# A four-layer image network: convolution copies, convolution taps, scan states and an elementwise sum change engines in its last layer

## The chip, the cores and the metric

The kernel runs on one core of a Trainium2 chip. The metric is the device time of one execution in microseconds (us), lower is better, given as the median of several runs. A core has five engines that run their own instruction streams side by side and wait for each other on semaphores: PE (TensorE, matrix products), DVE (VectorE), ACT (ScalarE), POOL (GpSimd) and SP (SyncE, which here issues DMAs). Data sits in SBUF (128 partitions), products land in PSUM, and DMA moves data between SBUF and device memory.

## The reference

The input is x of shape (2, 128, 128, 128), as batch, height, width and channels, in fp32. Four residual layers follow one another, each of the form x = x + layer(norm(x)). The first is windowed attention, the second a Fourier layer with a feed-forward part, the third a recurrent spectral layer of 16 steps. The change lies in the fourth, a selective-scan layer. Cut down, it computes:

```python
def layer3(x):                                  # x is already normalised
    xc, z = split(x @ W_in.T)                   # 256 channels each
    xc = silu(depthwise_conv3x3(xc, conv_w) + conv_b)
    # four sequences of 16384 pixels: 16 windows of 32 x 32, walked by
    # rows, by columns, and both of these backwards
    xs = stack([rows(xc), cols(xc), rows(xc)[::-1], cols(xc)[::-1]])
    dt, B, C = split(x_proj_w @ xs)             # 8, 16 and 16 rows
    delta = softplus(dt_proj_w @ dt + dt_proj_b)
    h = 0                                       # 256 channels x 16 states per sequence
    for t in range(16384):                      # for each of 2 batches x 4 directions
        h = exp(delta[t] * A) * h + delta[t] * xs[t] * B[t]
        y[t] = (h * C[t]).sum(over states) + xs[t] * Ds
    y = y_rows + y_rows_back + y_cols + y_cols_back    # each put back in pixel order
    y = layernorm(y) * ln_w + ln_b
    return (y * silu(z)) @ W_out.T
```

## The kernel before

Everything is fp32. The fourth layer has three stages, one after another, each with its own pools of tiles; a pool's number is how many buffers a tile name has, and a tile that needs a buffer waits until its last user is done.

**Convolution, `layer3_conv`.** It loops over 2 batches x 4 blocks of 32 image rows (`hg`), eight blocks in all. The order of instructions on each engine in this stage is chosen by the framework's scheduler. For a block, SP loads rows of the layer's input (`x3l`, L1141), and ACT normalises them into `xpad`, a padded tile of 34 rows by 130 columns. Then for each half of the 256 channels (`e` = 0, 1): PE multiplies by the input projection `win` (`zps`) and ACT copies the result into `xz`, again padded. The nine offsets ("taps") of the 3x3 convolution are split. Taps 0 to 2 are done by PE: their weights are folded into the projection, `cw` = conv_w x win, so a product of `cw` with the shifted `xpad` gives the projected tap (`cps`, L1172, two matmuls of 512 columns a tap). Taps 3 to 8 are done by DVE, each with one `scalar_tensor_tensor` over 128x1024 (L1181), the first of them adding to `cps` and the others to `acc`. There are four such groups (`g`, 8 rows each) for a block and half. ACT applies bias and silu into `xw` (L1185), which is stored by windows (`wg`, four for a block). Last, for each window, three things leave for device memory: `xw` in row order (`xs[0]`), a copy in column order `xv` (`xs[1]`), and a transposed copy `xt` (`xst`) that PE makes with transposes (`xtps`, L1207) and ACT copies out of PSUM (L1212). The column-order copy is L1194, on POOL, 128x1024, two for a window, 64 in all; it reads with a stride of 32 elements. `cps`, `xv`, `xt` and `xtps` have two buffers each, `acc`, `xz` and `xw` three.

**Scan, `layer3_scan`.** The sequences are cut into 256 parts, eight chains of 32 parts (2 batches x 4 directions), and a part into 8 slots, so 2048 slots (`g`), each with four scans of 512 steps. The order of instructions is written out by hand (`with in_order(tc)`): on turn `g` the loop calls `exponentials(g + 1)` (ACT, `da`, L1531), `kept(g - 1)` (ACT copies the last states, L1610), `products(g + 2)` (`but`, on ACT and POOL), `weighted(g - 1)` (POOL multiplies by C, L1616), `tiles(g)` (PE transposes into `ups`, DVE scans, L1598) and `sums(g - 2)` (PE, L1569). `tiles` starts each chain by making a state tile and clearing it:

```python
            if (b, k) not in states:
                states[(b, k)] = two.tile([P, 32], F32, name=f"state_{b}_{k}", tag="state")
                nc.gpsimd.memset(states[(b, k)], 0.0)
```

The call of `weighted(g - 1)` comes ahead of `tiles(g)`, so the clearing (L1582) stands behind that multiplication in POOL's order.

**Output, `layer3_out`.** 64 tiles of four image rows (512 pixels), order again written by hand. On turn `m` it calls, in this order: `load(m + 4)`, `join(m + 2)`, `project(m - 1)`, `weigh(m)`, `gate(m + 1)`, `norm(m + 1)`, `normal(m + 2)`. `load` fetches the tile's input and two scan sums `y` and `y2`, six buffers each. `join` adds the two in place (L1681, POOL, 128x1024). `norm` is the layer norm: statistics on DVE (L1708, L1710), the reciprocal root on POOL (`rsqrt_of`, L51 and L52), and then subtracting and scaling on DVE in four instructions of 128x256 (L1714). `weigh` transposes on PE (`yTp`, L1725), scales on ACT (L1728) and multiplies by the gate on DVE (L1732). `gate` computes silu(z) (L1697 on PE, L1700 on ACT), `project` multiplies by W_out and adds the residual (L1741, L1743), and ACT copies the result out (L1747) and issues its store.

Of the kernel before, what the change touches and what calls it, by code (L numbers as in the profile page):

```python
# [9 lines left out]
F32 = mybir.dt.float32  # L10
AF = mybir.ActivationFunctionType
ALU = mybir.AluOpType
# [3 lines left out]
P = 128  # L16
NB = 2
# [10 lines left out]
def rows_of(handle, n, offset=0):  # L28

    return bass.AP(handle.tensor, handle.offset + offset, [[0, P], [1, n]])  # L30
# [1063 lines left out]
def layer3_conv(tc, cs, ins, x3, xs, xst, sc, sh):  # L1094

    nc = tc.nc
    MAT = (0, 1, 2)
    VEC = (3, 4, 5, 6, 7, 8)
    with ExitStack() as ctx:
        pool = lambda name, bufs, **kw: ctx.enter_context(tc.tile_pool(name=name, bufs=bufs, **kw))
        w = pool("l3a_w", 1)
        two = pool("l3a_two", 2)
        three = pool("l3a_three", 3)
        ps_t = pool("l3a_ps_t", 2, space=PSUM)  # L1110
        ps_z = pool("l3a_ps_z", 2, space=PSUM)
        ps_c = pool("l3a_ps_c", 2, space=PSUM)
        win = w.tile([P, 256], F32, name="win")
        nc.sync.dma_start(win, ins["winT"][:, 0:256])

        cw = w.tile([P, len(MAT), 256], F32, name="cw")
        nc.sync.dma_start(cw.rearrange("p t e -> p (t e)"), rows_of(ins["conv_w_t"], len(MAT) * 256))

        cv = w.tile([P, 9, 2], F32, name="cv")
        nc.sync.dma_start(cv.rearrange("p t e -> p (t e)"), cols_of(ins["conv_w_t"], 9 * 256))  # L1120
        cb = w.tile([P, 2], F32, name="cb")
        nc.sync.dma_start(cb, cols_of(ins["L3_conv_conv_b"], 256))
        nc.vector.tensor_tensor(
            cw, cw, win.unsqueeze(1).to_broadcast([P, len(MAT), 256]), ALU.mult
        )
        for b in range(NB):
            for hg in range(4):
                xpad = two.tile([P, 34, 130], F32, name=f"xpad_{b}_{hg}", tag="xpad")
                nc.gpsimd.memset(xpad[:, :, 0:1], 0.0)  # L1129
                nc.gpsimd.memset(xpad[:, :, 129:130], 0.0)  # L1130
                if hg == 0:
                    nc.gpsimd.memset(xpad[:, 0:1, 1:129], 0.0)
                if hg == 3:
                    nc.gpsimd.memset(xpad[:, 33:34, 1:129], 0.0)
                r = max(32 * hg - 1, 0)
                end = min(32 * hg + 33, HW)
                while r < end:
                    n = min(8, end - r)
                    xl = two.tile([P, 8, HW], F32, name=f"x3l_{b}_{hg}_{r}", tag="x3l")
                    nc.sync.dma_start(  # L1140
                        xl[:, 0:n, :].rearrange("c r w -> c (r w)"), x3[b, :, r * HW : (r + n) * HW]  # L1141
                    )
                    p0 = r - 32 * hg + 1
                    nc.scalar.activation(
                        xpad[:, p0 : p0 + n, 1:129], xl[:, 0:n, :], AF.Identity,
                        bias=sh[:, b : b + 1], scale=sc[:, b : b + 1],
                    )
                    r += n
                xw = []
                for e in range(2):  # L1150
                    t = f"{b}_{hg}_{e}"
                    ep = slice(e * P, (e + 1) * P)
                    xz = three.tile([P, 34, 130], F32, name=f"xz_{t}", tag="xz")
                    nc.gpsimd.memset(xz[:, :, 0:1], 0.0)
                    nc.gpsimd.memset(xz[:, :, 129:130], 0.0)
                    for r in range(0, 34, 4):
                        n = min(4, 34 - r)
                        zps = ps_z.tile([P, 4, HW], F32, name=f"zps_{t}_{r}", tag="zps")
                        nc.tensor.matmul(
                            zps[:, 0:n, :], win[:, ep], xpad[:, r : r + n, 1:129],  # L1160
                            start=True, stop=True,
                        )
                        nc.scalar.copy(xz[:, r : r + n, 1:129], zps[:, 0:n, :])
                    xwe = three.tile([P, 4, 32, 32], F32, name=f"xw_{t}", tag="xw")
                    xw.append(xwe)
                    for g in range(4):
                        cps = ps_c.tile([P, 8, HW], F32, name=f"cps_{t}_{g}", tag="cps")
                        for i, tap in enumerate(MAT):
                            dy, dx = tap // 3, tap % 3
                            for h in range(2):  # L1170
                                r = 8 * g + 4 * h + dy
                                nc.tensor.matmul(  # L1172
                                    cps[:, 4 * h : 4 * h + 4, :], cw[:, i, ep],
                                    xpad[:, r : r + 4, dx : dx + HW],
                                    start=(i == 0), stop=(i == len(MAT) - 1),
                                )
                        acc = three.tile([P, 8, HW], F32, name=f"acc_{t}_{g}", tag="acc")
                        for i, tap in enumerate(VEC):
                            dy, dx = tap // 3, tap % 3
                            r = 8 * g + dy  # L1180
                            nc.vector.scalar_tensor_tensor(  # L1181
                                acc, xz[:, r : r + 8, dx : dx + HW], cv[:, tap, e : e + 1],
                                cps if i == 0 else acc, ALU.mult, ALU.add,
                            )
                        nc.scalar.activation(  # L1185
                            xwe[:, :, 8 * g : 8 * g + 8, :].rearrange("p g r w -> p r g w"),
                            acc.rearrange("p r (g w) -> p r g w", w=32),
                            AF.Silu, bias=cb[:, e : e + 1],
                        )
                for wg in range(4):  # L1190
                    t = f"{b}_{hg}_{wg}"
                    xv = two.tile([P, 2, 32, 32], F32, name=f"xv_{t}", tag="xv")
                    for e in range(2):
                        nc.gpsimd.tensor_copy(xv[:, e], xw[e][:, wg].rearrange("p h w -> p w h"))  # L1194
                        nc.sync.dma_start(
                            xs[0, b, hg, wg, :, e, :], xw[e][:, wg].rearrange("p h w -> p (h w)")
                        )
                        nc.sync.dma_start(
                            xs[1, b, hg, wg, :, e, :], xv[:, e].rearrange("p w h -> p (w h)")
                        )  # L1200
                    xt = two.tile([P, 8, 256], F32, name=f"xt_{t}", tag="xt")
                    for g in range(4):
                        tps = ps_t.tile([P, 2, 2, P], F32, name=f"xtps_{t}_{g}", tag="x3t")
                        for j in range(2):
                            for e in range(2):
                                h0 = 4 * (2 * g + j)
                                nc.tensor.transpose(  # L1207
                                    tps[:, j, e, :],
                                    xw[e][:, wg, h0 : h0 + 4, :].rearrange("p h w -> p (h w)"),
                                    cs.ident,  # L1210
                                )
                        nc.scalar.copy(  # L1212
                            xt[:, 2 * g : 2 * g + 2, :], tps.rearrange("p j e d -> p j (e d)")
                        )
                    nc.sync.dma_start(xst[b, hg, wg].rearrange("(t p) d -> p t d", p=P), xt)


def layer3_scan(tc, cs, ins, xs, xst, yc, ys):
# [11 lines left out]
    nc = tc.nc  # L1230
    NS, DR, NX, T = 16, 8, 40, 512
    with ExitStack() as ctx:
        pool = lambda name, bufs, **kw: ctx.enter_context(tc.tile_pool(name=name, bufs=bufs, **kw))
        w = pool("l3b_w", 1)
        one = pool("l3b_one", 1)
        two = pool("l3b_two", 2)
# [19 lines left out]
        for i in range(2):  # L1256
            t = w.tile([65, T], F32, name=f"xd{i}")
# [18 lines left out]
            for s in (range(15, -1, -1) if back else range(16))  # L1276
            for sub in ((1, 0) if back else (0, 1))
        ]
        states = {}
        held = {}  # L1280

        def tag_of(i):
# [291 lines left out]
        def tiles(g):  # L1574
            i, s = divmod(g, 8)
            q, e = divmod(s, 2)
            b, k, _, _ = parts[i]
            rev = k >= 2
            v = held[i]
            if (b, k) not in states:  # L1580
                states[(b, k)] = two.tile([P, 32], F32, name=f"state_{b}_{k}", tag="state")
                nc.gpsimd.memset(states[(b, k)], 0.0)  # L1582
            state = states[(b, k)]
            da = v.pop(("da", s))
            hs = three.tile([P, 4, T], F32, name=f"hs_{tag_of(i)}_{s}", tag="hs")
# [57 lines left out]
def layer3_out(tc, cs, ins, x3, ys, out, sc, sh):  # L1643
# [3 lines left out]
    nc = tc.nc  # L1647
    D = 256
    T = 4 * HW
    with ExitStack() as ctx:  # L1650
        pool = lambda name, bufs, **kw: ctx.enter_context(tc.tile_pool(name=name, bufs=bufs, **kw))
        w = pool("l3c_w", 1)
# [25 lines left out]

        def join(m):
            v = held[m]  # L1680
            nc.gpsimd.tensor_tensor(v["y"], v["y"], v["y2"], ALU.add)  # L1681

        def normal(m):
            v = held[m]
# [186 lines left out]
```

## Time and profile before

| | us |
|---|---|
| median of 3 runs | 18746.11 |
| lowest and highest run | 18732.81, 18746.66 |
| profiled execution | 18730.61 |
| span of its trace | 18728.8 |

| engine | busy, whole span |
|---|---|
| PE matmul | 14598.5 us, 78% |
| DVE | 16075.3 us, 86% |
| ACT | 14826.2 us, 79% |
| POOL | 12241.3 us, 65% |

The profile comes from one execution, whose own time is 15.5 us below the median of the runs. Its mean granted TensorE clock is 0.915 of full speed. Positions in it are in us from the start of the span. The stages of the fourth layer lie so: first convolution tap on DVE at 5734.6 and last one ended at 6309.8; first scan at 6379.5; scan until about 18072; output from about 18090 to the end.

Lines of the profile name the source line, the engine, the operation, and the tiles as "out<-in" with partitions x elements. In a group, "xN | busy, mean" gives the number of instructions, their busy time in us and the mean of one in ns, then the idle time of the engine just before them and what ended it. In a timeline the first number is the start, the second the length; square brackets hold the idle time before and its releaser.

### The profile page before, as it was taken

Reading aid. Unit: us, or ns where it says so; the run is one execution under the profiler, and the core shown is the slowest. Engines: PE = TensorE matmul, PEld = TensorE weight load, DVE = VectorE, ACT = ScalarE, POOL = GpSimd, SP = SyncE. Lnnn points to the kernel's source line nnn. Section 1 sums busy time; section 2 is a strip of 40 time slices with the busy share of each in tenths; the row PEclk is TensorE's granted clock in tenths of the full one; section 3 lists DMA queues with packets and bytes.
Section 4 is the critical chain, followed back from the end, with each engine's and each line's share of the span. In section 5 each row is a group of like instructions: output and inputs, shape, how many; then the busy total and the mean of one; then the engine's idle time right before and its main releaser. Section 6 shows DMA issues by size and latency. Waiting matters only on the chain. (4 is left out here: it accounts for less than half of the span.)

```text
span 18728.8 us, 280494 instructions
## 1 busy us (share of the span) xinstructions
PE 14598.5 (78%) x99066; PEld 8519.3 (45%) x99066; DVE 16075.3 (86%) x20635; ACT 14826.2 (79%) x30077; POOL 12241.3 (65%) x6845
## 2 busy tenths in 40 slices
PE   7888888887567777777777777777777777777777
PEld 5665666664223344444444444444444444444445
DVE  6666666336888899999999999999999999999986
ACT  4665666334453599999999999999999999999974
POOL 0000000011001599999999999999999999999973
PEclk9999999888779899999999999999999999999988
DMA  2000000121114444454445444544445444444544
GB/s 49 22 23 23 16 16 17 59 66 55 55 47 154 158 120 114 117 131 130 124 114 120 119 125 125 130 120 116 115 124 134 125 118 119 120 119 125 130 139 147
DMA packets 1228554, 1861.34 MB, mean 99 GB/s; under 512 B 120781, under 2 KB 587469, under 8 KB 1224846
## 3 DMA queue, kind: packets, MB, share of 16 engines
q1 hardware_dynamic: 1157374, 1817.40, 36.8%
q10 hardware_dynamic: 69776, 26.00, 0.6%
q8 instruction: 786, 12.88, 0.3%
q14 instruction: 618, 5.06, 0.1%
HBM read 1398.48 MB, written 444.60 MB: 98 GB/s over the span
## 5 line engine op out<-in xcount | busy, mean ns | idle before, releaser
L1598 DVE TENSOR_TENSOR_SCAN hs<-da,state,ups 128x512 f32<-128x512 f32 x8192 | 9917.7, 1261 | 284.5 <-PE ups L1590 221.8
L1616 POOL TENSOR_TENSOR hs<-hs,cb 128x2048 f32<-128x2048 f32 x2048 | 9386.2, 4583 | 350.3 <-POOL but L1550 160.8
L1590 PE MATMUL ups<-ident,but 128*128 128x128 f32 x32768 | 5562.6, 301 | 2629.5 <-DVE hs L1598 1769.1
L1590 PEld LDWEIGHTS ups<-ident,but 128*128 128x128 f32 x32768 | 3855.6, 150 | 6223.1 <-DVE hs L1598 3598.9
L1555 ACT ACTIVATE but<-du,bt 128x256 f32<-128x256 f32 x12800 | 5328.7, 497 | 4.5 <-DVE du L1436 4.2
L1531 ACT ACTIVATE da<-db,na 128x512 f32<-128x512 f32 x8192 | 5224.2, 710 | 21.3 <-DMA db<-dd 18.8
L1569 PE MATMUL yps<-hs,sel 128*32 128x512 f32 x16384 | 2482.9, 682 | 56.4 <-POOL hs L1616 43.0
L1550 POOL TENSOR_TENSOR but<-du,bt 128x256 f32<-128x256 f32 x3584 | 2147.3, 619 | 17.9 <-issue 17.9
L282 POOL TENSOR_TENSOR xres<-xres,rowb 128x256 f32<-128x256 f32 x128 | 93.3, 729 | 2650.0 <-DMA xres<-in_x 2496.9
L390 ACT COPY pT<-tps 128x512 f32<-128x512 f32 x1280 | 723.7, 586 | 1125.1 <-PE tps L385 1125.1
L385 PE MATMUL tps<-ident,s 128*128 128x128 f32 x8192 | 1183.7, 283 | 367.5 <-DVE pT L388 272.8
L358 DVE CUSTOM_DVE_ANT_0 s<-sps,relbias 128x512 f32<-128x512 f32 x2048 | 1321.3, 682 | 112.4 <-PE sps L342 106.9
L385 PEld LDWEIGHTS tps<-ident,s 128*128 128x128 f32 x8192 | 890.5, 142 | 897.9 <-issue 484.9
L370 ACT ACTIVATE s<-s,nm 128x1024 f32<-128x1024 f32 x1024 | 1163.5, 1137 | 84.7 <-DVE nm L368 81.4
L1129 POOL MEMSET xpad<- 128x34 f32 x8 | 1.3, 162 | 1252.3 <-PE xs L1021 1178.9
L1610 ACT COPY state<-hs 128x4 f32<-128x4 f32 x2048 | 381.0, 186 | 295.7 <-DVE hs L1598 295.7
L342 PE MATMUL sps<-kc,qT 32*128 32x512 f32 x4096 | 593.9, 647 | 0.8 <-DVE nm L358 0.8
L388 DVE COPY pT<-tps 128x512 f32<-128x512 f32 x768 | 526.8, 686 | 58.5 <-PE tps L385 58.0
L1569 PEld LDWEIGHTS yps<-hs,sel 128*32 128x32 f32 x16384 | 339.5, 114 | 481.5 <-issue 308.2
L1319 PE MATMUL xdps<-xc,xpw 128*40 128x512 f32 x1024 | 540.8, 610 | 15.1 <-POOL xd L1259 15.1
L725 POOL TENSOR_TENSOR xr<-xr,row_ln_b 128x512 f32<-128x512 f32 x64 | 81.2, 1270 | 705.9 <-DMA xr<-x 289.1
L1351 PE MATMUL dtps<-xd,dtw 65*128 65x512 f32 x1024 | 529.8, 599 | 0.0
(286 smaller groups left out, 17249.4 us busy)
## 6 DMA issues: line engine op xcount, KB each, us to landing
db<-dd SPq DMA_DIRECT2D x1024, 512.0 KB
cb<-cd SPq DMA_DIRECT2D x1024, 256.0 KB
xc<-xs SPq DMA_DIRECT2D x256, 512.0 KB
dd<-dl SPq DMA_DIRECT2D x256, 512.0 KB
ut<-xst SPq DMA_DIRECT2D x128, 512.0 KB
yc<-ysb SPq DMA_DIRECT2D x128, 512.0 KB
yf<-yc SPq DMA_DIRECT2D x128, 512.0 KB
ys<-yt SPq DMA_DIRECT2D x128, 512.0 KB
```

Of the source, the lines that this page charges most:

```text
L342: nc.tensor.matmul(sps, v["qT"][hp, qt * P : (qt + 1) * P], kc[b, wh + g][hp, :, c0 : c0 + 32], start=True, stop=True,)
L358: nc.vector.tensor_tensor_reduce(v["s", qt][:, h, cols], v["sps", qt, g][h], bias[:, qt, h, cols], op0=ALU.add, op1=ALU.min, scale=-1.0, s ...
L370: nc.scalar.activation(s[:, h, :], s[:, h, :], AF.Exp, bias=nm[:, 2, h : h + 1], scale=-1.0, accum_out=v["sums"][:, qt, h : h + 1],)
L385: nc.tensor.transpose(tps[:, j, :], v["s", qt][:, h, k0 : k0 + P], cs.ident)
L390: nc.scalar.copy(dst, tps)
L1531: nc.scalar.activation(da[:, j, :], held[i]["db"][:, 4 * e + j, :], AF.Exp, scale=na[:, k, c : c + 1])
L1550: nc.gpsimd.tensor_tensor(but[:, j, :, n, :], du[:, tb], bt[:, tb, c : c + 1].unsqueeze(2).to_broadcast([P, 8, 32]), ALU.mult,)
L1555: nc.scalar.activation(but[:, j, :, n, :], du[:, tb], AF.Copy, scale=bt[:, tb, c : c + 1])
L1569: nc.tensor.matmul(v["yps"][e][32 * j : 32 * j + 32, :], sel, hs[:, j, :], start=(q == 0), stop=(q == 3),)
L1590: nc.tensor.transpose(ups[:, tb * P : (tb + 1) * P], v[("but", q, tb // 2)][:, tb % 2, 4 * e + j].rearrange("p n c -> p (n c)"), cs.ident,)
L1598: nc.vector.tensor_tensor_scan(o, a, u, state[:, c0 + j : c0 + j + 1], ALU.mult, ALU.add)
L1616: nc.gpsimd.tensor_tensor(hs, hs, v["cb"][:, s // 2, :].unsqueeze(1).to_broadcast([P, 4, T]), ALU.mult)
```

## The change

There are four edits, all in the fourth layer.

1. The column-order copies `xv` (L1194) move from POOL to ACT.
2. The split of the taps depends on the channel half: 3 taps on PE and 6 on DVE for `e` = 0, and 2 on PE and 7 on DVE for `e` = 1. DVE has 416 tap instructions in place of 384; PE has 640 matmuls of `cps` in place of 768.
3. The scan has one tile of states for all eight chains, cleared once on POOL ahead of the loop, in place of a tile and a clearing for each chain.
4. `join` moves from POOL to DVE. Its place in the loop stays.

```diff
 def layer3_conv(tc, cs, ins, x3, xs, xst, sc, sh):
-    MAT = (0, 1, 2)
-    VEC = (3, 4, 5, 6, 7, 8)
+    MATS, TAPS = (3, 2), 9
+    most = max(MATS)
...
-                        for i, tap in enumerate(MAT):
+                        for tap in range(MATS[e]):
                             dy, dx = tap // 3, tap % 3
                             for h in range(2):
                                 r = 8 * g + 4 * h + dy
                                 nc.tensor.matmul(
-                                    cps[:, 4 * h : 4 * h + 4, :], cw[:, i, ep],
+                                    cps[:, 4 * h : 4 * h + 4, :], cw[:, tap, ep],
                                     xpad[:, r : r + 4, dx : dx + HW],
-                                    start=(i == 0), stop=(i == len(MAT) - 1),
+                                    start=(tap == 0), stop=(tap == MATS[e] - 1),
                                 )
                         acc = three.tile([P, 8, HW], F32, name=f"acc_{t}_{g}", tag="acc")
-                        for i, tap in enumerate(VEC):
+                        for tap in range(MATS[e], TAPS):
                             dy, dx = tap // 3, tap % 3
                             r = 8 * g + dy
                             nc.vector.scalar_tensor_tensor(
                                 acc, xz[:, r : r + 8, dx : dx + HW], cv[:, tap, e : e + 1],
-                                cps if i == 0 else acc, ALU.mult, ALU.add,
+                                cps if tap == MATS[e] else acc, ALU.mult, ALU.add,
                             )
...
                     for e in range(2):
-                        nc.gpsimd.tensor_copy(xv[:, e], xw[e][:, wg].rearrange("p h w -> p w h"))
+                        nc.scalar.copy(xv[:, e], xw[e][:, wg].rearrange("p h w -> p w h"))
...
 layer3_scan:
-        states = {}
+        zero = w.tile([P, NB, 4, 32], F32, name="states")
+        nc.gpsimd.memset(zero, 0.0)
+        states = {(b, k): zero[:, b, k] for b in range(NB) for k in range(4)}
...
         def tiles(g):
-            if (b, k) not in states:
-                states[(b, k)] = two.tile([P, 32], F32, name=f"state_{b}_{k}", tag="state")
-                nc.gpsimd.memset(states[(b, k)], 0.0)
             state = states[(b, k)]
...
 layer3_out:
         def join(m):
             v = held[m]
-            nc.gpsimd.tensor_tensor(v["y"], v["y"], v["y2"], ALU.add)
+            nc.vector.tensor_tensor(v["y"], v["y"], v["y2"], ALU.add)
```

More of the change, by code (lines that the diff above doesn't have):

```diff
@@ L1114, in layer3_conv @@
         nc.sync.dma_start(win, ins["winT"][:, 0:256])
-        cw = w.tile([P, len(MAT), 256], F32, name="cw")
-        nc.sync.dma_start(cw.rearrange("p t e -> p (t e)"), rows_of(ins["conv_w_t"], len(MAT) * 256))
+        cw = w.tile([P, most, 256], F32, name="cw")
+        nc.sync.dma_start(cw.rearrange("p t e -> p (t e)"), rows_of(ins["conv_w_t"], most * 256))
         cv = w.tile([P, 9, 2], F32, name="cv")
@@ L1123, in layer3_conv @@
         nc.vector.tensor_tensor(
-            cw, cw, win.unsqueeze(1).to_broadcast([P, len(MAT), 256]), ALU.mult
+            cw, cw, win.unsqueeze(1).to_broadcast([P, most, 256]), ALU.mult
         )
```

## The prediction

> **What bounds the kernel now.** The change touches three stretches of the span: the convolution (5715 to 6345 us), the scan (6379 to 18072) and the output stage (18090 to 18729). I read the busy table by stretch, then the groups, waits and timeline of each.
>
> The busy table (stretch, its length, then busy us and instructions by engine, TensorE's clock, DMA share, GB/s):
>
> ```profile
> 5715.00:6360.00 645.00, 548.05 (x1587) 262.73 (x1588) 543.28 (x396) 258.74 (x383) 162.82 (x109) 0.91 0.52 187
> 18100.00:18690.00 590.00, 442.65 (x2160) 311.75 (x2160) 375.12 (x781) 238.39 (x360) 217.84 (x182) 0.85 0.53 162
> ```
>
> The convolution keeps PE and DVE busy side by side; ACT and POOL have room. DVE works from 5734.6 to 6309.8, 543 of 575 us, so it sets the pace with PE close behind. In the output stage no engine is full: a chain of waits from tile to tile sets it. Groups of the convolution:
>
> ```profile
> L1181 DVE SCALAR_TENSOR_TENSOR acc<-xz,cv,acc 128x1024 f32<-128x1024 f32 x320 | 462.1, 1472 | 7.6 <-DVE acc L1181 0.5
> L1172 PE MATMUL cps<-xpad,cw 128*128 128x512 f32 x768 | 353.9, 603 | 0.8 <-DVE acc L1181 0.8
> L1194 POOL COPY xv<-xw 128x1024 f32<-128x1024 f32 x64 | 156.2, 2475 | 106.6 <-ACT xw L1185 90.6 <-issue 14.7 <-POOL xv L1194 1.0
> ...
> L1181 DVE SCALAR_TENSOR_TENSOR acc<-xz,cv,cps 128x1024 f32<-128x1024 f32 x64 | 81.6, 1275 | 45.2 <-PE cps L1172 35.2 <-POOL xv L1194 10.0
> ```
>
> The taps on `acc` average 1472 ns, those on `cps` 1275. The timeline tells why (start, length, engine):
>
> ```profile
> 5933.38 8.83 DVE L1181 SCALAR_TENSOR_TENSOR acc<-xz,cv,acc 128x1024 f32<-128x1024 f32 x7
> ...
> 5944.59 12.00 DVE L1181 SCALAR_TENSOR_TENSOR acc<-xz,cv,acc 128x1024 f32<-128x1024 f32 x5
> 5956.50 1.27 DVE L1181 SCALAR_TENSOR_TENSOR acc<-xz,cv,cps 128x1024 f32<-128x1024 f32 x1
> ```
>
> POOL's four `xv` copies lie at 5943.46 to 5954.2: the five taps beside them take 2.40 us each instead of 1.26. Undisturbed runs elsewhere come at 1.21 us apiece (six in 7.26 at 5746.99). The longest `acc` form takes 3.10 us, the longest `cps` form 1.28.
>
> In the scan DVE, ACT and POOL are all busy about 97% of a window. One stall belongs to the change; the DVE wait list has it seven times, and the timeline shows one:
>
> ```profile
> DVE hs L1598 <- POOL state L1582: 50.2, 7, 8.0
> ```
> ```profile
> 16611.20 4.53 POOL L1616 TENSOR_TENSOR hs<-hs,cb 128x2048 f32<-128x2048 f32 x1
> ...
> 16614.73 2.54 ACT L1531 ACTIVATE da<-db,na 128x512 f32<-128x512 f32 x4
> 16615.66 0.13 POOL L1582 MEMSET state<- 128x32 f32 x1
> ...
> 16615.83 4.79 DVE L1598 TENSOR_TENSOR_SCAN hs<-da,state,ups 128x512 f32<-128x512 f32 x4 [7.09 <-POOL state L1582]
> ...
> 16620.71 0.20 ACT L1610 COPY state<-hs 128x4 f32<-128x4 f32 x1 [3.43 <-DVE hs L1598]
> ```
>
> A 0.13 us memset stands in POOL's order behind a 4.53 us multiplication; the scans wait for it. Output stage, tile 61 and then 62:
>
> ```profile
> 18697.74 2.34 POOL L1681 TENSOR_TENSOR y<-y,y 128x1024 f32<-128x1024 f32 x1
> 18697.80 3.39 DVE L1714 TENSOR_SCALAR y<-y,mv,rs 128x256 f32<-128x256 f32 x4 [1.47 <-POOL rs L52]
> ...
> 18700.38 2.20 PE L1725 MATMUL yTp<-ident,y 128*128 128x128 f32 x8 [2.39 <-DVE y L1714]
> ...
> 18703.43 1.22 DVE L1732 TENSOR_TENSOR yT<-yT,z 128x1024 f32<-128x1024 f32 x1 [2.23 <-ACT yT L1728]
> ...
> 18707.72 1.38 DVE L1714 TENSOR_SCALAR y<-y,mv,rs 128x256 f32<-128x256 f32 x4 [1.47 <-POOL rs L52]
> ...
> 18708.28 1.65 PE L1725 MATMUL yTp<-ident,y 128*128 128x128 f32 x8 [0.21 <-DVE y L1714]
> ```
>
> With a join beside it the normalisation takes 3.39 us; for the last tiles, whose joins are over, 1.38. The trace so holds the experiment already: `yTp` of tiles 0 and 61 are at 18103.62 and 18700.38, 9.78 us a tile; the last two tiles follow after 7.90 and 7.57.
>
> [...] L1714 and the two-input taps stretch beside POOL, the `cps` taps, with one SBUF input, never. [...]
>
> **Part 1, copies to ACT and taps to DVE.** Before: 320 × 1.21 = 387 us of the 462 is work, 75 is stretch, nearly half of POOL's 156. After: 416 taps, 64 on `cps`, so 352 × 1.21 + 64 × 1.275 = 508. To it come DVE's idle 32 us, less the 10 that it waits for POOL, and nothing more from PE: its 384 products become 320, in 512-column matmuls 768 to 640, and its busy time per block of rows (eight blocks) falls from 64 to about 57 us, under DVE's 63.5. 530 against 575 is **−45**. If the new pace exposes PE, 10 more.
>
> ACT takes 64 copies. No row shows an ACT copy that reads in column order; its ends are 1.06 us (contiguous, L1363) and 1.95: a strided write, L687, takes 1031 ns for 512 elements against 585, so 0.87 ns an element more. [...] I take 1.9. ACT per block is then 32 + 8 × 1.9 = 47 us, inside 63. The copies also wait for the landing of the `xs` DMA of two windows earlier (their number stays at 64 on SP's queue, where a late copy holds up the `x3l` loads queued behind its store; those run two blocks ahead, so I cost that at nothing), a wait that POOL bore before; two such waits a block, with `silu` and `xt` copies queued behind on ACT, and behind those the transposes and `cps` products on PE. DVE's backlog and 16 us of ACT's room cover some. After the last tap the tail grows by about 4 us (eight copies of 1.9 replace POOL's, beside 16 `xt` copies). Sum **−40**, between −65 (no idle at all) and +10 (each landing wait exposed by some 3 us).
>
> **Part 2, states zeroed once.** Seven stalls, 50.2 us. Without the memset the scans at 16615.83 start at 16608.8 (`da` of that slot is done at 16610.28, its first quarter earlier), but the next slot's `da` begins at 16614.73, so DVE waits for it about 1.8 us: 5.5 gained at most. ACT, as full as DVE, loses only its 3.43 us at L1610. I take the middle, 4.4 × 7 = **−31**, between −15 and −50. One 128x256 memset ahead of the scan lies beside the loads: nothing.
>
> **Part 3, join on DVE.** It stands behind L1714 of one tile and ahead of L1732, in the 1.90 to 2.23 us that DVE waits there for ACT. At 1.22 us (L1732's shape) it fits; its operands were loaded two tiles ahead. L1714 goes to 1.38, and POOL keeps only L51 and L52 between tiles. Cycle: the mean of 7.90 and 7.57, 7.74; (9.78 − 7.74) × 61 = **−124**. Bounds: all at 7.57, −135; +0.5 us a tile because the join delays L1732 or the loads (1.57 MB a tile, 161 GB/s now, 203 then; 18100 to 18150 already shows 202), −95.
>
> **Sum.** −40 −31 −124 = −195. The profiled execution took 18730.61 us (span 18728.8), which becomes 18535.6; it is 15.5 under the median 18746.11, so the median forecast is **18551 us**.
>
> **Rivals.** 0.2% (37 us) is about what a measurement of this kernel can tell from no change.
> 1. ACT's queue eats part 1's gain: strided copies above 1.95 us or landing waits of about 10 us. For it: ACT already waits 23.1 us for `xs` landings at L1185. Against: 16 us of room per block. 18551 + 49 = 18600.
> 2. Something else holds the output tile: DMA at 165 to 175 GB/s, or PE's clock (0.85 there). Cycle 9.2, so part 3 gives 35 instead of 124: 18640. Against it: the early 202 GB/s.
> 3. The scan's stall returns as waiting on ACT's `da` or PE's `ups` (199 us of such waits already): 18582.
> 4. The stretch isn't POOL's doing, so the change doesn't do what it says: joins and copies gain nothing, 32 more taps cost 39, the scan gives 31: about 18754, unchanged. Against it: tiles 62 and 63, and the 1.28 limit of the `cps` taps.
> 5. Slower: the landing waits on ACT. Each holds `silu`, `xt`, PE's transposes and `cps`, and so DVE. Beyond about 8 us a wait the 16 us of room per block are gone, and each further us costs 16 (16 waits in all). The −195 and the bound (37) are eaten from some 22 us a wait (232 / 16 + 8); at 25 the waits cost 272, which gives 18551 + 272 = 18823. Against: the longest such wait on a transfer in this stage is 11.6 us.
>
> **Numbers.** Forecast 0.62 (own range 18510 to 18590), rival 1 0.16, rival 2 0.10, rival 3 0.06, rival 4 0.03, rival 5 0.03. Faster 0.94, same 0.03, slower 0.03. Range: down to all low bounds (−65 −50 −135, 18496), taken as 18490; up past rivals 1 and 2, 18645.
>
> **What would show it.** Right: no `acc` tap over 1.3 us, DVE's taps about 508 us; ACT copies near 1.9; no wait on a state memset; L1714 at 400 ns each, L1732's wait under 1 us, 7.7 us between tiles. Wrong: long ACT waits for `xs` landings with DVE waiting for `cps`; a cycle above 9 with engines idle; the scan's end moved by under 15 us.

## The result, and the profile after

| | before | changed |
|---|---|---|
| median, us | 18742.08 | 18492.42 |
| lowest and highest run | 18732.81, 18746.66 | 18486.78, 18498.69 |
| profiled execution | 18730.61 | 18497.56 |

Four runs of each stand behind these medians; the forecast started from the median of the first three runs of the kernel before, 18746.11. The change takes 250 us off; the ratio is 0.9867, with a 95% interval of 0.985 to 0.9885. A later repeat beside the kernel before gave 0.9869 (0.9856 to 0.9883). I had forecast 195 us and a range that ended at 18490, so the run came in 2 us inside the edge of the range, for reasons that the experiments separate.

The stages, from the two profiled executions (us), which lie 233 us apart:

| | before | changed | difference |
|---|---|---|---|
| first tap of the convolution on DVE | 5734.6 | 5730.4 | −4 |
| first to last tap | 575.2 | 504.6 | −71 |
| last tap to first scan | 69.6 | 67.4 | −2 |
| first scan to first transpose of the output stage | 11724 | 11702 | −22 |
| first to last transpose of the output stage, 63 tiles on | 613.6 | 479.3 | −134 |

The start of the convolution lay between 5725 and 5741 in all the traces of this study, so the first row says nothing.

The busy table by stretch, of the changed kernel (stretch, length, busy us and instructions of PE, PE's weight loads, DVE, ACT and POOL, then TensorE's clock, DMA share, GB/s):

```profile
5715.00:6360.00 645.00, 536.34 (x1716) 250.06 (x1714) 560.89 (x479) 436.28 (x575) 55.60 (x75) 0.92 0.58 200
18000.00:18480.00 480.00, 397.01 (x2253) 283.36 (x2254) 336.95 (x885) 239.26 (x376) 79.67 (x126) 0.99 0.66 202
```

In the first stretch POOL has gone from 163 us to 56 and ACT from 259 to 436; the first line also holds the beginning of the scan, which now starts inside it. In the second the transfers go at 202 GB/s, where they went at 162, and TensorE's granted clock is 0.99, where it was 0.85. Groups of the convolution in the changed kernel:

```profile
L1182 DVE SCALAR_TENSOR_TENSOR acc<-xz,cv,acc 128x1024 f32<-128x1024 f32 x352 | 426.6, 1278 | 0.3
...
L1195 ACT COPY xv<-xw 128x1024 f32<-128x1024 f32 x64 | 127.6, 2043 | 0.6 <-DMA xs<-xv 0.5
...
L1182 DVE SCALAR_TENSOR_TENSOR acc<-xz,cv,cps 128x1024 f32<-128x1024 f32 x64 | 81.6, 1275 | 19.4 <-PE cps L1173 15.6 <-ACT xw L1186 3.5
```

The taps on `acc` are down from 1472 to 1278 ns, the length that the undisturbed ones had (1281 ns by the mean of the 266 that overlap no `xv` copy in the trace of before). There are 32 more of them, yet they cost 36 us less in all (462.1 us before). The 508 us of taps fill the 504.6 us from end to end (neighbours overlap a little in the records). Of the 19.4 us of waits on the last line, 14 lie before the first tap. The copy in column order costs 2.04 us on ACT, and the wait for the landing of older stores that I feared is 0.5 us in the whole stage.

VectorE's waits in the scan of the changed kernel (6330 to 18000):

```profile
DVE hs L1599 <- PE ups L1591: 214.8, 408, 1.7
...
DVE hs L1599 <- ACT da L1535: 3.1, 2, 1.6
```

The seven waits on a cleared state are gone, and ScalarE has not taken their place: 3.1 us on `da`. The waits for `ups` were 201.9 us before (6385 to 18072), so about 13 us came back there. Why the stage is then only 22 us shorter is told below. One tile of the output stage in the changed kernel:

```profile
18300.47 1.38 DVE L1715 TENSOR_SCALAR y<-y,mv,rs 128x256 f32<-128x256 f32 x4 [1.47 <-POOL rs L52]
...
18301.03 1.64 PE L1726 MATMUL yTp<-ident,y 128*128 128x128 f32 x8 [0.85 <-DVE y L1715]
18301.77 1.22 DVE L1682 TENSOR_TENSOR y<-y,y 128x1024 f32<-128x1024 f32 x1
...
18303.76 1.23 DVE L1733 TENSOR_TENSOR yT<-yT,z 128x1024 f32<-128x1024 f32 x1 [0.77 <-ACT yT L1729]
...
18308.05 1.38 DVE L1715 TENSOR_SCALAR y<-y,mv,rs 128x256 f32<-128x256 f32 x4 [1.47 <-POOL rs L52]
```

The normalisation takes 1.38 us, the join lies in the gap behind it, what is left of the gap is 0.77, and the next tile is 7.58 us on. Could the higher clock of TensorE have shortened the tile instead? By the medians of tiles 10 to 49 the tile went from 9.74 to 7.57 us. Of these 2.17 us the normalisation gives 2.02 (3.40 to 1.38), and the gap between it and the gate's product, in which PE and ScalarE work, gives 0.15 (2.05 to 1.90). The other steps of VectorE's chain have the lengths that they had. So little is left for the clock; why it rose is not shown.

### The profile page after: what moved, and what is told of

Same layout as the page of the kernel before. It is cut to its first block, busy times and chain, and to the rows that moved or that the text cites. A ratio compares the mean times of both kernels' runs of the same rounds, so it can differ in the third digit from the quotient of the medians.

```text
span 18495.8 us, 280256 instructions
## 1 busy us (share of the span) xinstructions
PE 14497.6 (78%) x98938; PEld 8455.1 (46%) x98938; DVE 15999.1 (87%) x20731; ACT 14932.9 (81%) x30141; POOL 11956.1 (65%) x6710
## 5 line engine op out<-in xcount | busy, mean ns | idle before, releaser
L1599 DVE TENSOR_TENSOR_SCAN hs<-da,states,ups 128x512 f32<-128x512 f32 x8192 | 9920.7, 1262 | 248.9 <-PE ups L1591 235.9
L1611 ACT COPY states<-hs 128x4 f32<-128x4 f32 x2048 | 380.9, 186 | 274.9 <-DVE hs L1599 274.7
```

What stands on the lines that cost most here:

```text
L1599: nc.vector.tensor_tensor_scan(o, a, u, state[:, c0 + j : c0 + j + 1], ALU.mult, ALU.add)
```

## The experiments

Each table gives medians and the ratio to the kernel before from runs on the same chip. Stage times are from each kernel's own trace.

**The four edits, one at a time.** Four kernels, each the kernel before with one of the edits of the change and nothing else.

```diff
join_only, in layer3_out:
-            nc.gpsimd.tensor_tensor(v["y"], v["y"], v["y2"], ALU.add)
+            nc.vector.tensor_tensor(v["y"], v["y"], v["y2"], ALU.add)
states_only, in layer3_scan:
-        states = {}
+        zero = w.tile([P, NB, 4, 32], F32, name="states")
+        nc.gpsimd.memset(zero, 0.0)
+        states = {(b, k): zero[:, b, k] for b in range(NB) for k in range(4)}
...
-                nc.gpsimd.memset(states[(b, k)], 0.0)
copies_only, in layer3_conv:
-                        nc.gpsimd.tensor_copy(xv[:, e], xw[e][:, wg].rearrange("p h w -> p w h"))
+                        nc.scalar.copy(xv[:, e], xw[e][:, wg].rearrange("p h w -> p w h"))
taps_only, in layer3_conv:
-    MAT = (0, 1, 2)
-    VEC = (3, 4, 5, 6, 7, 8)
+    MATS, TAPS = (3, 2), 9
```

> The kernel before with one edit: the join on VectorE. Theory (POOL's join stretches the normalisation beside it, and the join fits the gap ahead of the gate's product): the cycle of the output stage falls from 9.78 to about 7.6 us a tile, 125 to 135 us off the run, conv and scan as before; normalisation instructions near 0.40 us each. Rival (transfers or TensorE's clock hold the tile): cycle above 9, under 50 us off.

> The kernel before with one edit: states cleared once. Theory: each of seven chain starts saves about 7 us (49 in all), and what is given back is a number of 4 us hitches, where the up<-ae instruction of VectorE starts just after POOL's long multiplication; the changed kernel's trace had 10 of them, before's 3. So 20 to 50 us off, and the sum of switches and hitches in the trace equals the gain. Rival (ScalarE sets the pace, only its 3.4 us a switch are gained): 24 us with the hitches as in before.

> The kernel before with one edit: the column-order copies on ScalarE, 3 and 6 taps for both halves. Theory A: VectorE's stretch (75 us) goes, but with 768 matmuls of cps PE (513 us busy for the stage) then sets the pace: the stage shrinks by 30 to 50 us, and VectorE waits for cps. Theory B: VectorE's work (469 us) sets it: the stage shrinks by 75 to 100 us and the split of taps was not needed.

> The kernel before with one edit: 3 and 2 taps as matrices, copies still on POOL. Theory: VectorE has 508 us of work and about 75 of stretch beside POOL's copies, 583 against 575 before, and no more waits for cps: the stage is 0 to 20 us longer. Rival (most of the stage's gain came from fewer matmuls): 20 us or more off.

| | median, us | against before (18751.2) | ratio, 95% interval | first to last tap |
|---|---|---|---|---|
| join_only | 18614.77 | −136 | 0.9927 (0.9914 to 0.9939) | 574.1 |
| states_only | 18701.81 | −49 | 0.997 (0.9959 to 0.9982) | 575.5 |
| copies_only | 18693.7 | −57 | 0.997 (0.9958 to 0.9982) | 524.0 |
| taps_only | 18760.01 | +9 | 1.0002 (0.9994 to 1.001) | 577.0 |

*The join* gives what it gives in the whole change: 7.59 us from one tile's transposes to the next, against 9.72 before. *The states* give 49 us, the length of the seven stalls. *The copies* follow theory A (51 us off the stage, where its upper edge was 50). The groups of copies_only in the convolution:

```profile
L1181 DVE SCALAR_TENSOR_TENSOR acc<-xz,cv,acc 128x1024 f32<-128x1024 f32 x320 | 401.1, 1282 | 7.7 <-DVE acc L1181 0.5
L1181 DVE SCALAR_TENSOR_TENSOR acc<-xz,cv,cps 128x1024 f32<-128x1024 f32 x64 | 81.7, 1277 | 54.0 <-PE cps L1172 50.8 <-ACT xv L1194 3.3
```

The stretch is gone, but VectorE now waits for `cps`: between first and last tap the list of waits has

```profile
DVE acc L1181 <- PE cps L1172: 36.6, 20, 3.5
```

*The taps* alone leave the stretch where it was. The same group in taps_only:

```profile
L1182 DVE SCALAR_TENSOR_TENSOR acc<-xz,cv,acc 128x1024 f32<-128x1024 f32 x352 | 505.2, 1497 | 0.3
L1182 DVE SCALAR_TENSOR_TENSOR acc<-xz,cv,cps 128x1024 f32<-128x1024 f32 x64 | 81.2, 1269 | 14.2 <-PE cps L1173 14.2
```

It has no wait for PE inside the stage (the 14.2 lie before the first tap), and 1497 ns a tap. So the two edits of the convolution are not additive: −51 and +2 alone, −71 together. The copies take away the stretch and then run into PE; the other split of the taps moves 128 matmuls off PE and is worth nothing until the copies have left POOL. The four medians sum to −233, against −250 and −242 (in the repeat) for the whole change. The rest has the sign of this interaction, which is 22 us by the stage times; the intervals don't separate it.

**Is it the join's place, or POOL's traffic?** The changed kernel, with a sum of the same shape put back on POOL; it reads other data and nobody reads its result.

```diff
             nc.vector.tensor_tensor(v["y"], v["y"], v["y2"], ALU.add)
+            idle = two.tile([P, 4, D], F32, name=f"idle_{m}", tag="idle")
+            nc.gpsimd.tensor_tensor(idle, <first half of v["xl"], repeated>, <second half, repeated>, ALU.add)
```

> The changed kernel with a sum of 128x1024 added on POOL at the place that the join had, on other operands (the two halves of the tile's residual input), into a tile that nobody reads; the join stays on VectorE. Theory (it is POOL's traffic beside the normalisation that costs, not who does the join): the normalisation goes back to about 3.4 us a tile and the cycle from 7.6 to 9.6 us or more, 120 to 160 us longer than the changed kernel. Rival (the cost was the join's own place in the chain of its tile): no change.

Measured: 18631.93, ratio to before 0.9936 (0.9924 to 0.9949), so 120 to 130 us of the gain are lost again. The cycle is 9.73 us. The output stage of pool_sum has

```profile
L1717 DVE TENSOR_SCALAR y<-y,mv,rs 128x256 f32<-128x256 f32 x248 | 208.9, 901 | 91.4 <-POOL rs L52 91.4
```

901 ns, where the changed kernel has 408. Which engine does the join did not matter by itself here: VectorE does it in 1.22 us of a wait that it had anyway, and a POOL sum that no one waits for costs nearly all that the move had gained.

**What bounds the convolution now?** Two variants of the changed kernel.

```diff
taps22:
-    MATS, TAPS = (3, 2), 9
+    MATS, TAPS = (2, 2), 9
copies_twice:
-                        nc.scalar.copy(xv[:, e], xw[e][:, wg].rearrange("p h w -> p w h"))
+                        for _ in range(2):
+                            nc.scalar.copy(xv[:, e], xw[e][:, wg].rearrange("p h w -> p w h"))
```

> The changed kernel with 2 and 2 taps as matrices: 32 more taps on VectorE, 128 matmuls fewer on PE. Theory (VectorE is now the bound of the convolution, with no wait left): 32 x 1.2 = 38 us longer than the changed kernel. Rival (PE holds it): shorter, or within 10 us.

> The changed kernel with each column-order copy on ScalarE made twice, 64 x 2.0 = 128 us more of ScalarE work, 16 us a block of rows. Theory (ScalarE has that much room): the stage is 0 to 30 us longer. Rival (ScalarE's queue holds silu and xt back, and so VectorE): 60 us or more, with VectorE waiting for cps or for a free acc.

taps22: 18521.43, ratio 0.9874 (0.9861 to 0.9888). By medians it is about 29 us longer than the first median of the changed kernel, which the intervals alone don't separate; its stage does: 536.2 us between first and last tap against 504.6, 32 us for 32 taps. At 1.21 us they are 39 us; the changed kernel has 5 us of waits between first and last tap (1.6 for `cps`, 3.5 for `xw`), and taps22 has none. VectorE is the bound.

copies_twice: 18612.79, ratio 0.9925 (0.9911 to 0.9939), and 604.9 us between first and last tap, 100 longer. The theory of 16 us of room a block of rows fell: of 128 us of added ScalarE work 100 came through. VectorE's waits in the stage of copies_twice (14.1 us of the last line lie before the first tap):

```profile
DVE acc L1182 <- issue: 49.8, 4, 13.1
DVE acc L1182 <- ACT xw L1186: 47.4, 8, 14.0
DVE acc L1182 <- PE cps L1173: 20.6, 7, 14.1
```

ScalarE is still not full (432 of 565 us, 5770 to 6335). Its copies come in a batch, here sixteen for a block with the `xt` copies among them, and `silu` of the next block stands behind the batch; VectorE runs out of `acc` buffers and stops up to 14 us at a time. What the 49.8 us without a releaser wait for, the trace does not say. The changed kernel's own 3.5 us of waits for `xw` are of the same kind; together with the 100 of 128 us they suggest, but don't show, that it lies close to this edge.

**Where did the gain of the states go in the first trace?** The start of ACT's Exp (L1363 before, L1367 after) of each of the 256 parts gives the lead of the changed kernel along the scan. At the seven chain starts it grows by 7.4, 7.0, 7.6, 7.3, 7.4, 6.8 and 7.7 us, 51 in all. Between them it jumps back by 4 us several times, where one part takes 4.0 us longer than its 45.4. One such place in the changed kernel, and the same place one part later:

```profile
11784.65 4.52 POOL L1617 TENSOR_TENSOR hs<-hs,cb 128x2048 f32<-128x2048 f32 x1 [0.82 <-POOL but L1554]
11784.76 4.96 DVE L1373 TENSOR_SCALAR up<-ae 128x1024 f32<-128x1024 f32 x1
```
```profile
11833.81 0.67 DVE L1373 TENSOR_SCALAR up<-ae 128x1024 f32<-128x1024 f32 x1
...
11834.05 4.83 POOL L1617 TENSOR_TENSOR hs<-hs,cb 128x2048 f32<-128x2048 f32 x1 [0.81 <-POOL but L1554]
```

`up<-ae` is the + 1 of the softplus, a one-source operation from SBUF. In the first case POOL's multiplication began 0.11 us ahead of it, and it took 4.96 us instead of 0.67. In the second `up<-ae` was ahead by 0.24 us, and only the multiplication was stretched a little (4.83 us; 4.56 by the median of all 2048). So a third of a microsecond decides 4 us here. The count of such parts, chain starts apart, differs from trace to trace whether or not the change is in: 3 before, 10 after, 5, 8, 12 and 12 in states_only, join_only, copies_only and taps_only. Ten against three is 28 us of the 51 given back in this pair of traces.

The ten are of two kinds. In four of them (`up<-ae` at 9646, 11785, 15618 and 16801) the operation starts 0.11 to 0.13 us behind the multiplication and takes 4.94 to 4.97 us. This kind is no chance: the same four parts are caught in the traces of after_again, pool_sum, copies_twice and norm_split, and the kernel before, join_only and copies_only share two others. The other six look like this:

```profile
7947.60 1.92 PE L1355 MATMUL dtps<-xd,dtw 65*128 65x512 f32 x2
...
7950.48 1.28 DVE L1599 TENSOR_TENSOR_SCAN hs<-da,states,ups 128x512 f32<-128x512 f32 x1 [1.28 <-PE ups L1591]
...
7956.44 2.57 DVE L1373 TENSOR_SCALAR up<-ae 128x1024 f32<-128x1024 f32 x1
```

From 7945 to 7950 TensorE's granted clock is 0.50, and the two `dtps` products take 1.92 us where they take 1.02 at 9733.77, with a granted clock of 1.00. In all six parts two to four of the part's four `dtps` products take 1.06 us each; in the other four parts none takes over 0.60. In these six parts VectorE stands idle for 3.1 to 4.6 us in the 13.5 us ahead of `up<-ae` (0.24 by the median of all parts), so it is late for the multiplication, and loses 1.2 to 1.9 us more behind it. Only one of the three parts of before is of this kind. Which parts meet a stretch of half clock changes in part from run to run of the same kernel, and the number of such parts doesn't follow the change: 1 to 10 in the four traces with the seven clearings, 3 to 7 in the seven without them and with `up<-ae` in its old place. So 5 of the 7 extra parts, some 20 us, go with the clock and not with the change, and 2, some 8 us, with where the changed program happens to put `up<-ae`. In all of these parts `up<-ae` ends 5.07 to 5.12 us after the multiplication's start, whether it began 0.1 or 3.3 us into it.

All these traces together give the worth of the states cleared once. From first scan to first transpose of the output stage the four with the seven clearings take 11724 to 11764 us, and the other seven 11684 to 11709. With 4 us taken off for each late part these become 11707 to 11716 and 11660 to 11667: about 50 us apart. Two kernels move `up<-ae` alone within its slot; a third run repeats the changed kernel:

```diff
up_later:
-            (-7, "head", softplus_a), (-7, 0, turned_b), (-7, 2, softplus_b),
+            (-7, "head", softplus_a), (-7, 0, turned_b), (-7, 3, softplus_b),
up_earlier:
+            (-7, "head", softplus_a), (-7, 0, turned_b), (-7, 1, softplus_b),
```

> The changed kernel with the softplus step up<-ae on VectorE (tensor_scalar, both operands in SBUF) one place later in its slot, behind the third scan. Theory of the 4 us hitches (an up<-ae that starts after POOL's long multiplication has begun waits for nearly all the rest of it): now it starts inside that multiplication in most of the 256 parts and takes 3 to 4 us each time, 300 to 750 us longer. Rival (hitches come from elsewhere): within 30 us.

> The changed kernel as it is, as the measure for the other three of this call: about 18490 to 18500 us. The number of 4 us hitches in its scan, where up<-ae is caught behind POOL's multiplication, should differ from the 10 of its first trace if it is chance.

> The changed kernel with up<-ae one place earlier in its slot, ahead of the scan after which it stood. Theory (POOL's long multiplication starts at about the moment at which up<-ae used to start; 1.2 us earlier it is never caught): no hitch of 4 us in the scan, 20 to 45 us less than the changed kernel. Rival (at the new place it meets POOL's shorter products or waits for ScalarE's ae): within 15 us, or longer.

up_later: 19172.22, ratio to before 1.0223 (1.0209 to 1.0237): 680 us longer than the changed kernel, for moving 256 instructions by one scan. They now start about 0.93 us into the multiplication. Its group over the scan:

```profile
L1373 DVE TENSOR_SCALAR up<-ae 128x1024 f32<-128x1024 f32 x251 | 1028.4, 4097 | 0.0
```

Nearly every one is caught now. after_again: 18499.6, 11 late parts: the same four that are caught at full clock, and seven at half clock, four of these at other places than in the first trace. up_earlier: 18479.31, ratio 0.9861 (0.9847 to 0.9874), 20 us under after_again with overlapping intervals; 3 parts longer by about 5 us instead of 11 by 4, all three at half clock. The four fixed catches are gone. The place is not free either: `up<-ae` averages 1190 ns there (775 in the changed kernel). In the trace of the changed kernel a place 1.19 us earlier lies beside POOL's short `but` products (two in 1.22 us at 11832.02); that they are what stretches it is my estimate. The expectation of no late part at all missed.

**A better version.** In the output stage VectorE still waits twice a tile, 1.47 us for POOL's root and 0.77 for ScalarE. norm_split gives it another tile's work there; best has up_earlier's move too.

```diff
+            held[m]["mr"] = (mv, rstd)
+        def scaled(m):
+            y = held[m]["y"]
+            mv, rstd = held[m].pop("mr")
             for r in range(4):
                 nc.vector.tensor_scalar(
...
-                for lag, step in ((-4, load), (-2, join), (1, project), (0, weigh), (-1, gate), (-1, norm), (-2, normal)):
+                for lag, step in ((-4, load), (-1, norm), (1, project), (0, weigh), (-1, gate), (-2, join), (-1, scaled), (-2, normal)):
```

> The changed kernel with the output stage's norm cut in two: statistics and root of tile m+1 ahead of the gate's product of tile m, then the join of m+2, then the normalisation of m+1. VectorE's two waits of a tile (1.47 us for POOL's root, 0.77 for ScalarE's yT) get work of another tile. Theory: the cycle falls from 7.6 us to between 6.3 and 6.6, where PE's work of a tile (6.3 us) sets it: 60 to 80 us less than the changed kernel. Rival (the transfers, 1.57 MB a tile, 245 GB/s at 6.4 us, set it): 7.0 us or more.

> Both: up<-ae earlier and the norm cut in two. The two lie in different stages, so the gains add: 80 to 125 us less than the changed kernel, about 18370 to 18415.

norm_split: 18439.96, ratio 0.9837 (0.9823 to 0.985), 6.59 us a tile. Two lines of its list of waits in the output stage:

```profile
POOL rs L51 <- DVE mv L1711: 319.6, 61, 6.5
...
DVE yT L1738 <- ACT yT L1734: 80.3, 61, 1.4
```

POOL waits for VectorE's statistics, and the list has no wait of VectorE for the root any more. One of 1.31 us a tile for ScalarE's `yT` is left. The transfers ran at 234 GB/s, and the list has 0.2 us of waits for them. best: 18423.13, ratio 0.9832 (0.9819 to 0.9846), 76 us under after_again, whose interval (0.9856 to 0.9883) it does not touch. It misses the lower edge that I gave for the gain (80) by 4; by medians norm_split gives 60 of it, the move of `up<-ae` the rest. The forecast of 18370 to 18415 for best missed by 8.

## Why the prediction was right or wrong

**The direction and the main mechanism were right.** All three stages moved for the reasons given: POOL's work beside them stretched VectorE's instructions (pool_sum restores it: 901 ns for 408), the clearing held the scans (states_only), and the join fitted its gap (join_only). What stretches beside POOL is measured. In the trace of before the 54 taps on `acc` that overlap an `xv` copy average 2.41 us, the other 266 take 1.28; of the taps on `cps` 20 overlap a copy, and none of these takes more than 1.28. The normalisation takes 3.39 us beside a join and 1.38 without, so the number of SBUF inputs alone doesn't tell them apart: it has one, as have the taps on `cps`. In the scan `up<-ae` takes 4.96 us behind POOL by 0.11, 0.67 ahead of it by 0.24, and every late `up<-ae` ends 5.1 us after POOL's 4.5 us multiplication began. What the two engines contend for, no trace here shows.

**The sum was too small: −195 forecast, −250 measured**, just under my own range for the likeliest case (18510 to 18590). Two waits were priced wrongly, and that the run stayed 2 us inside the whole range is in part luck: the late parts hid some 28 us in the profiled pair, and each one fewer would have taken 4 us off. Term by term:

- *Taps at 1.21 us and the 75 us of stretch*: right. 352 × 1.21 gives 426, the group shows 426.6.
- *The 22 us of idle that I kept*: wrong, and the largest miss. I had taken PE off the critical path by my own working (57 us a block under 63.5) and still kept the waits for it from the trace of before. copies_only shows 36.6 us of waits for `cps` with 768 matmuls, the changed kernel under 2 inside the stage with 640. The stage gave 71, not 45.
- *The tail, +4*: it was −2 in this pair of traces, and 0 in most others with the copies on ScalarE (69.5 to 70.0 us against 69.6). The ACT copies cost 2.04 us, a little above the 1.9 that I took, my estimate between the two ends, and the 1.95 that I gave as the upper one, so the price was not what failed.
- *The switch of a chain, 4.4 us*: wrong. I had DVE stop again for `da` and ACT pace the gain. The trace shows 6.8 to 7.7 a switch and 3.1 us of waits on `da` in the whole scan. states_only's −49 against my −31 is that term; in the profiled pair itself the late parts left only −22.
- *The join, −124*: a tile takes 7.58, not 7.74. Of the two steps between tiles at the end, 7.57 was the typical one. The 7.90 still had the end of a stretched tile in it: VectorE waited 2.23 us ahead of L1732 there, and 1.90 in the next. Measured −134 between the transposes, −136 by join_only's median.

**The rivals.** ScalarE's queue (rival 1) did not eat the gain, though the copies did take longer than its 1.95 us. My argument against it, 16 us of room a block, was wrong: in copies_twice 100 of 128 us of added work came through. Rival 2 fell: the output stage moved 202 GB/s, then 234 in norm_split, and the clock, 0.85 before, leaves about 0.15 us a tile at most, as worked out above. Rival 3 fell: 3.1 us of waits on `da` and some 13 more on `ups` stand against the 50 that went. Rival 4 fell with pool_sum and copies_only. Rival 5, the waits for landings, came to 0.5 us; its threshold of 22 us a wait rests on the same 16 us of room and was not tested.

## What to carry to other kernels

When an instruction's duration varies from row to row, look at what the other engines do beside it, and price the edit from the undisturbed rows of the same trace: here they gave the new time of the taps and of the output tile to about 2%. When a bound moves, ask of every old wait whether its cause is still there; keeping the average of before is a hidden assumption. An engine's free share of a stage is no cover if its work comes in batches with other engines' inputs queued behind: in copies_twice ScalarE was busy for 432 of 565 us, and 100 of 128 us of added work came through.

## What the runs showed that I had not expected

`up<-ae`, a VectorE operation of 0.67 us (one SBUF source, 128x1024), costs 4.1 us on average when it starts 0.9 us into POOL's 4.5 us multiplication; 256 of these made the program 680 us slower. In the scan of the changed kernel the two engines start a few tenths of a microsecond apart, and a shift from 0.24 us ahead to 0.11 behind costs 4 us. Some of these losses are fixed by the program (the same four parts in five traces). More of them came with stretches in which TensorE ran at a granted clock of 0.50, in which VectorE fell behind by 3.1 to 4.6 us of idle time: 3 to 12 late parts a trace in these kernels with `up<-ae` in its old place, and they hid half of a 51 us gain in the first pair of traces.

A POOL operation that no one waits for, on an engine that has little else to do there (80 us busy of 480 in the changed kernel), cost 2.1 us a tile on another engine (pool_sum).
